# Blocks for the second token group, nine products ahead of the first, and largest logits spread through memory, with a new plan of places and ranks

## The chip, the cores and the metric

The kernel runs on one core of one Trainium2 chip. The metric is the device time of one execution in microseconds (us): less is better. Three runs of the kernel before took 664.44, 664.75 and 665.0 us, so the median is 664.75. The core's TensorE clock as granted was 0.997 of full speed in the profiled execution.

The engines are named as the profile names them: PE (TensorE, matrix products), DVE (VectorE), ACT (ScalarE), POOL (GpSimd) and SP (SyncE, which here only issues transfers).

## What is computed

All values are f32. x is [4, 2048, 256]: 4 sequences of 2048 tokens. Cut to what matters, the reference is:

```
q, k, v = gelu(x W1 + b1) W2 + b2            # three small MLPs, 256 wide
scores  = tril(q k^T) / scale                # no softmax
out     = layernorm(scores v) * ln_w + ln_b
x       = layernorm(x + out)
xn      = layernorm(x) * gamma + beta
logits  = unit(xn) . unit(mu)                # 256 columns: 16 experts x 16 slots
dispatch = softmax(logits, over the tokens of a sequence)
combine  = softmax(logits, over the 256 columns)
slot_in  = dispatch^T xn ; h = gelu(slot_in w1 + b1) ; slot_out = h w2 + b2
x        = layernorm(x + combine slot_out)
```

The attention is linear, so it can be run as a sum that is carried along (k^T v). The dispatch softmax needs, for each of the 256 columns, the largest logit over all 2048 tokens of a sequence. The code keeps logits with their sign turned, so it looks for the least.

## The kernel before

**Tiling.** Tokens are taken in 16 groups of 512 (4 chunks of 128 partitions), 4 groups to a sequence. For each group t, attend (L774) brings x into a transposed form xT, makes q, k and v, the products of k and q, the running state and the attention output; norms (L1018) does the layer norms; back (L1137) makes the logits and the combine weights. After the fourth group of a sequence, softmaxes (L1232) and slots (L1333) do the dispatch and the experts, and finish (L1447) adds the result for each of the four groups and stores it.

**How the order of work is made.** Nothing is run where it is written. Each piece of work is a step of a planner (class Plan, L56): an engine, a length, what it reads and writes, and a rank. The rank is the base given by the last plan.begin(...) plus 0.01 for each step, and it is less by 1.5 for a step that reads a PSUM bank (L93). Plan.run (L119) plays the steps with these lengths and with lateness by engine (LATE, L58; PATIENCE, L61, says how much a rank weighs against being ready, for SP alone), and emits them in the order that comes out. Each engine then runs its own list in that order and waits on semaphores. Buffers are handed out in the same play from a number of places for each tag (L263 to L292): for example hid 5 (the gelu outputs of q, k and v), vt 1, kt 1, xT 2. PSUM has three sets of banks (L299 to L301): mm 3, tp 2, at 3.

**The start.** load_x (L304) loads a group of x as rows. For t of 2 and more it also loads the same group by blocks, 8 transfers of 64 KB each (emit_blocks, L330), which attend turns into xT with one DVE transposition (L782). For groups 0 and 1 attend transposes the rows on PE instead (transpose_group, L489, whose PE step is L481), and copies the two banks with DVE (L471) and ACT (L472). Weights arrive by transfers issued at once (load_weights, L368); the planner is told when to expect them by the list of arrivals. The expert weights w1, w2 and b2 are queued on SP (load_experts, L389). fold (L723) joins W2q and W2k: transpositions of both on PE (L733), copies (L741), three products (L755), and three evictions on DVE (L765) into wqk_sb, which the kt products (L820) read. unit_mu (L686) scales mu; it uses spread.

**A group.** PE makes q, k and v (L797, two tiles of 512 columns each), ACT applies gelu (L807), then the kt products (L820, evicted by DVE at L830) and v's second product (L847, evicted at L858). kt is turned through memory: stored by SP (turn_out, L507, issue at L513), read back in blocks (turn_in, L518, issue at L522) and transposed on DVE (L529) before its products with q (L872). The carried state is L899 (evicted at L915), the column sums are L932, which ACT copies (L941), SP stores (L947) and reads back for all partitions (L952, L956). The outputs are L982 and L986. The logits are L1166, their running least is mx (L1188).

**The end of a sequence.** softmaxes transposes mx on PE (L1241), DVE reduces it to cm, two columns of 128 partitions (L1249), and spread (L666) brings these 256 values to all partitions: DVE multiplies the identity by each column (L672), PE multiplies a matrix of ones by that (L678), ACT copies the bank (L1266). POOL then subtracts it from the logits of each group (L1277; SUBTRACT at L23 says which engine for the very last group's chunks), ACT applies Exp (L1289), and the slot sums on PE (L1311) contract over all tokens. The experts are L1363, L1387, L1406 and L1433, the last product is L1537 (combine, L1530), added by DVE at L1545. For the last two sequences finish_by_sums (L1504) gets the norm from an accumulated sum and a square on ACT (L558), then a root on POOL (root_of, L565: L573, L582, L587, L588, L589), then a centering on ACT (L604) or DVE (L609), as CENTERS (L21) says. PIECES (L19) cuts the last group into chunks; the piece marked True is normed by finish_own (L1461) with DVE's own statistics (L548, L549), a root on POOL (L537) and a centering at L1480. store is L1490.

The last sequence is treated apart: its first three groups are summed early (part_sums), and spread is called for them and once more for the last group.

Of the kernel before, what the change touches and what calls it, by code (L numbers as in the profile page):

```python
# [14 lines left out]
P = 128  # L15
G = 4
ACCZ = 14

PIECES = ((2, False), (2, True))  # L19

CENTERS = [['ACT', 'ACT', 'ACT', 'ACT'], ['ACT', 'DVE', 'DVE', 'DVE'], ['ACT', 'ACT', 'ACT', 'ACT'], ['DVE', 'DVE', 'DVE', 'DVE'], ['ACT', 'DVE', 'ACT', 'DVE'], ['ACT', 'DVE', 'DVE', 'DVE'], ['ACT', 'ACT', 'ACT', 'ACT'], ['DVE', 'DVE', 'ACT', 'DVE']]  # L21

SUBTRACT = ['DVE', 'POOL', 'DVE', 'POOL']  # L23

TAIL = {'norms': 0, 'back': 0.3, 'softE': 1.4, 'part': 2.2, 'soft': 1.0, 'slots2': 4.6, 'fin2': [5.5, 0.3], 'slots3': 1.7, 'fin3': [2.6, 0.2], 'table': 1.0}
LAST = 2
# [29 lines left out]
class Plan:  # L56
# [1 line left out]
    LATE = {"PE": 0.45, "DVE": 0.25, "ACT": 0.25, "POOL": 0.25, "SP": 3.5, "IN": 0.0}  # L58
    TABLE = 1.3

    PATIENCE = {"PE": 0.0, "DVE": 0.0, "ACT": 0.0, "POOL": 0.0, "SP": 1.0, "IN": 0.0}  # L61

    def __init__(self):
        self.steps, self.places, self.order, self.free = [], {}, {}, set()
# [155 lines left out]
def kernel(  # L220
# [36 lines left out]
        plan.tag(tag, tiles, free=math.prod(shape) < 32 or tag == "ct")  # L257

    def bank_places(tag, n):
        plan.tag(f"ps_{tag}", [banks.tile([P, 512], F32, name=f"{tag}_{i}") for i in range(n)], True)  # L260

    for tag, n, shape in (
        ("row", 8, [G, C + 1]),  # L263
        ("xT", 2, [KC, W]),
        ("hid", 5, [KC, W]),
        ("kT", 1, [KC, W]),
        ("vt", 1, [G, C]),
        ("kt", 1, [G, C + 1]),
        ("sT", 1, [G, P]),
        ("a", 2, [G, C]),  # L270
        ("run", 2, [C]),
        ("cs", 1, [C]),
        ("state", 3, [KC, C]),
        ("xn", 2, [G, C]),
        ("xnT", 1, [KC, W]),
        ("lg", 7, [G, ES]),
        ("mx", 1, [ES]),
        ("ct", 5, [EH, W]),
        ("dg", 1, [EH, P]),
        ("si", 1, [EH, C]),  # L280
        ("siT", 1, [KC, ES]),
        ("hp", 1, [NP, S]),
        ("st", 7, [G, 6]),
        ("mv", 14, [G, 2]),
        ("ve", 10, [G]),
        ("root", 24, [G]),
        ("ss", 6, [G]),
        ("nrm", 4, [G]),
        ("sum", 12, [G]),
        ("re", 12, [G]),  # L290
        ("rc", 6, [1]),
        ("cm", 6, [EH]),  # L292
    ):
        places(tag, n, shape)
    plan.tag(
        "bounce", [memory.tile([KC, W, P], F32, name=f"bounce_{i}") for i in range(16)], True
    )
    plan.tag("sums", [memory.tile([G, C], F32, name=f"sums_{i}") for i in range(2)], True)
    bank_places("mm", 3)  # L299
    bank_places("tp", 2)  # L300
    bank_places("at", 3)  # L301


    x_tiles, xs_tiles = {}, {}  # L304

    def load_x(t):
        if t >= ngroups:
            return
        b, g = divmod(t, NG)
        xt = plan.buffer("row", G)  # L310

        def emit():
            nc.sync.dma_start(
                out=xt[:, :, :C],
                in_=x[b, g * W : (g + 1) * W, :].rearrange("(c p) d -> p c d", p=P),
            )
            if t == 0:
                load_weights()
            if t == 1:
                load_rows()  # L320

        plan.step("SP", {0: 2.5, 1: 6.0, 2: 4.0}.get(t, 0.5), emit, writes=[xt])
        x_tiles[t] = xt
        if t < 2:
            return


        xs = plan.buffer("xT", KC)

        def emit_blocks():  # L330
            xb = x[b, g * W : (g + 1) * W, :].rearrange(
                "(n c) (k a r) -> a c k n r", c=32, k=KC, r=32
            )
            for a in range(P // 32):
                for k in range(KC):
                    nc.sync.dma_start(
                        out=xs[32 * a : 32 * (a + 1), k, :].rearrange(
                            "c (n r) -> c n r", r=32
                        ),
                        in_=xb[a][:, k],  # L340
                    )

        plan.step("SP", 4.8, emit_blocks, writes=[xs])
        xs_tiles[t] = xs
# [72 lines left out]

    arrivals = {}
    for n, after in (
        ("W1q", 7.0), ("W1k", 0.5), ("W1v", 1.0), ("muw", 0.5), ("W2q", 0.5), ("W2k", 0.5),  # L420
        ("W2v", 1.0), ("rows", 4.0),
    ):
        plan.tag(n, [mu_sb])
        arrivals[n] = plan.buffer(n)
        plan.step("IN", after, lambda: None, [], [arrivals[n]])
# [28 lines left out]
        pattern=[[1, P]],  # L454
        channel_multiplier=-1,
    )

    hz_t = const.tile([P, NP, 2, S], F32, name="hz")
    nc.gpsimd.memset(hz_t, 0.0)
# [772 lines left out]
    def softmaxes(groups, before=None):  # L1232
# [22 lines left out]
        if before:  # L1255
# [3 lines left out]
                nc.vector.tensor_tensor(less.place, cm.place, before.place, ALU.subtract)  # L1259

            plan.step("DVE", 0.3, emit, [before], [cm, less])
        row = spread(cm)
        cmb = plan.buffer("dg")
        plan.step(
            "ACT", _act(ES),
            lambda: nc.scalar.copy(cmb.place.rearrange("p h e -> p (h e)"), row[:, :ES]),  # L1266
            [row], [cmb],
        )
        for t in groups:

            n = 1 if t == ngroups - 1 else G
# [293 lines left out]
    for t in range(ngroups):  # L1565
# [3 lines left out]
        last = t == ngroups - 1  # L1569
        plan.begin(t)  # L1570
        attend(t)
        plan.begin(t + (TAIL["norms"] if last else 0.6))
        norms(t)
        plan.begin(t + 0.3)
        load_x(t + 2)
        plan.begin(t + (TAIL["back"] if last else 1.1))
        back(t)
        if t == ngroups - 2:

# [5 lines left out]
            kept = part_sums(early)  # L1585
        if t % NG == NG - 1:
            groups = [t] if tail == 2 else list(range(t - NG + 1, t + 1))
            plan.begin(t + (TAIL["soft"] if tail == 2 else 1.4))
            _, less = softmaxes(groups, cm if tail == 2 else None)
            plan.begin(t + (1.7, TAIL["slots2"], TAIL["slots3"])[tail])  # L1590
            so = slots(groups, kept if tail == 2 else None, less)
# [50 lines left out]
```

## Time and profile before

| what | value |
|---|---|
| median of three runs | 664.75 us |
| the profiled execution | 665.03 us |
| its span, first to last instruction | 663.3 us |
| PE busy | 645.4 us, 97% of the span |
| DVE, POOL, ACT busy | 493.4, 298.8, 266.3 us |
| transfers of the hardware queue q1 | 83.06 MB, 59.8% of what 16 DMA engines have in the span |
| first PE product | at 5.88 us |
| PE busy in 0 to 10, 10 to 20, 20 to 30, 30 to 40 us | 4.12, 10.0, 10.0, 9.36 us |
| DMA share in 10 to 20 and 20 to 30 us | 1.00 and 1.17 |
| PE busy from 650 us to the end | 5.63 us |

The span is counted from the first to the last instruction of the profiled execution; 1.7 us of that execution's time lie outside it. A line of the profile names the engine, the line of the code, the operation, the tiles out<-in with their shape, how often, the busy time and the time of one, and the idle time before it with what ended it. In the order of time, a line gives the start, the time that the merged run of like instructions spans, and in brackets the idle time of that engine before it. SPq and ACTq are the issues of transfers, which take the issuing engine's time only. PEld is the load of weights into PE, which runs beside products. An f32 product of the code shows as two records.

### The profile page before, as it was taken

The page shows a single profiled execution, that of the slowest core. Times are in us where ns is not written, and L with a number is a line of the kernel's source. Part 1 is how long each engine was busy: PE and PEld are TensorE (multiplying, and loading weights), DVE is VectorE, ACT ScalarE, POOL GpSimd, SP SyncE. Part 2 cuts the span into 40 slices and gives each one's busy share as a digit, 9 for nine tenths or more (in the row PEclk, how much of TensorE's full clock was granted, in tenths as well). Part 3 has the DMA queues.
Part 4 walks back from the last instruction along what each step waited for, and adds up shares of the span by engine and source line. Part 5 has one row for each costly group of instructions (what it writes and reads, how often), then busy time and mean ns, then how long its engine had stood idle before and what let it go on. Part 6 is the DMA issues. An engine that isn't in the chain of part 4 may idle for free.

```text
span 663.3 us, 9332 instructions
## 1 busy us (share of the span) xinstructions
PE 645.4 (97%) x2954; PEld 479.4 (72%) x2954; DVE 493.4 (74%) x1294; ACT 266.3 (40%) x597; POOL 298.8 (45%) x346
## 2 busy tenths in 40 slices
PE   6999999999999999999999999999999999999995
PEld 3757586777768877758686887776867768887874
DVE  1438586979797878878796388996969589886486
ACT  3130415243346227221516323624153545545475
POOL 3443516060739414353426605546061937646234
PEclk9999999999999999999999999999999999999998
DMA  8953655877677095836676425995677382621284
GB/s 245 261 118 103 139 91 133 128 151 153 108 152 128 8 212 164 189 88 128 127 142 123 87 64 95 234 211 104 111 149 132 70 159 68 84 65 32 33 159 159
DMA packets 322233, 84.71 MB, mean 128 GB/s; under 512 B 253068, under 2 KB 319944, under 8 KB 322184
## 3 DMA queue, kind: packets, MB, share of 16 engines
q1 hardware_dynamic: 321080, 83.06, 59.8%
q10 hardware_dynamic: 960, 0.80, 0.4%
q8 instruction: 23, 0.38, 0.2%
q0 software_dynamic: 144, 0.26, 0.1%
q14 instruction: 26, 0.21, 0.1%
HBM read 52.05 MB, written 32.04 MB: 127 GB/s over the span
## 4 chain that ended last, share of the span: by engine, by line
PE 91%; DVE 5%; issue 1%; DMA 1%; POOL 0%; POOLq 0%; ACT 0%; DVEq 0%; ACTq 0%
PE mm L797 25%; PE at L899 8%; PE mm L847 8%; PE mm L1166 8%; PE at L1537 7%; PE at L982 7%; PE mm L820 7%; PE at L1311 7%; PE at L872 4%; PE at L986 4%; PE at L932 1%; DVE mx L1188 1%; DMA row<-in_x_dram 1%; PE tp L481 1%; DVE xn L1091 1%
## 5 line engine op out<-in xcount | busy, mean ns | idle before, releaser
L807 ACT ACTIVATE hid<-mm,cols_sb 128x512 f32<-128x512 f32 x96 | 65.1, 687 | 139.2 <-PE mm L797 138.7
L537 POOL TENSOR_TENSOR root<-ve,nhalf 128x4 f32<-128x4 f32 (+1 forms) x39 | 40.6, 1041 | 127.8 <-DVE ve L1032 51.5
L982 PE MATMUL at<-state,hid 128*128 128x256 f32 x240 | 61.7, 379 | 0.0
L797 PE MATMUL mm<-xT,W1q_sb 128*128 128x512 f32 x128 | 61.3, 608 | 0.3 <-DVE xT L471 0.3
L899 PE MATMUL at<-vt,kt 128*128 128x256 f32 x240 | 61.4, 386 | 0.0
L820 PE MATMUL mm<-both_sb,hid 128*128 128x257 f32 x256 | 59.5, 381 | 1.3 <-DVE kt L830 1.3
L797 PE MATMUL mm<-xT,W1v_sb 128*128 128x512 f32 x128 | 59.4, 592 | 0.0
L1537 PE MATMUL at<-so,ct 128*128 128x256 f32 x256 | 58.0, 381 | 0.8 <-DVE row L1545 0.6
L1311 PE MATMUL at<-row,lg 128*128 128x257 f32 x256 | 58.2, 380 | 0.0
L847 PE MATMUL mm<-W2v_sb,hid 128*128 128x256 f32 x256 | 58.1, 379 | 0.0
L1166 PE MATMUL mm<-mu_sb,xnT 128*128 128x256 f32 x256 | 58.1, 379 | 0.0
L797 PE MATMUL mm<-xT,W1k_sb 128*128 128x512 f32 x128 | 57.8, 593 | 0.0
L1537 PEld LDWEIGHTS at<-so,ct 128*128 128x128 f32 x256 | 48.0, 190 | 10.0 <-issue 1.7
L820 PEld LDWEIGHTS mm<-both_sb,hid 128*128 128x128 f32 x256 | 48.2, 190 | 9.7 <-DVE kt L830 1.9
L1166 PEld LDWEIGHTS mm<-mu_sb,xnT 128*128 128x128 f32 x256 | 48.4, 190 | 8.4 <-issue 1.4
L1025 POOL TENSOR_TENSOR row<-row,rows_sb 128x1024 f32<-128x1024 f32 x16 | 35.1, 2196 | 42.7 <-DMA row<-in_x_dram 38.1
L982 PEld LDWEIGHTS at<-state,hid 128*128 128x128 f32 x240 | 45.5, 190 | 12.2 <-issue 6.0
L847 PEld LDWEIGHTS mm<-W2v_sb,hid 128*128 128x128 f32 x256 | 48.4, 190 | 6.9 <-DVE kt L830 0.3
L1311 PEld LDWEIGHTS at<-row,lg 128*128 128x128 f32 x256 | 48.1, 190 | 7.2 <-issue 0.4
L899 PEld LDWEIGHTS at<-vt,kt 128*128 128x128 f32 x240 | 44.3, 190 | 12.3 <-issue 5.4
L1216 POOL TENSOR_TENSOR sum<-sum,ss 128x4 f32<-128x4 f32 x16 | 4.0, 249 | 108.6 <-DVE ss L1212 92.2
L941 ACT COPY cs<-at 128x256 f32<-128x256 f32 (+1 forms) x16 | 5.9, 371 | 109.3 <-PE at L932 97.7
(148 smaller groups left out, 1247.5 us busy)
## 6 DMA issues: line engine op xcount, KB each, us to landing
bounce<-xn SPq DMA_DIRECT2D x30, 512.0 KB
row<-in_x_dram SPq DMA_DIRECT2D x16, 512.0 KB
ct<-bounce SPq DMA_DIRECT2D x64, 128.0 KB
bounce<-kt SPq DMA_DIRECT2D x30, 256.0 KB
kT<-bounce SPq DMA_DIRECT2D x60, 128.0 KB
out_dram<-row SPq DMA_DIRECT2D x15, 512.0 KB
xT<-in_x_dram SPq DMA_DIRECT2D x112, 64.0 KB
xnT<-bounce SPq DMA_DIRECT2D x56, 128.0 KB
```

Of the source, the lines that this page charges most:

```text
L537: nc.gpsimd.tensor_tensor(r[:, :n], v[:, :n], nhalf.to_broadcast([P, n]), ALU.pow)
L797: nc.tensor.matmul(ph.place, wa[f"W1{n}"][:, k, m * P : (m + 1) * P], xT[:, k, :], start=(k == 0), stop=(k == KC - 1),)
L807: nc.scalar.activation(hid[n][:, m, :], ph.place, AF.Gelu, bias=cols_sb[:, 4 * i + m : 4 * i + m + 1],)
L820: nc.tensor.matmul(pk[:, : C + 1], hid["k"][:, k, c * P : (c + 1) * P], wqk_sb[:, k, :], start=(k == 0), stop=(k == KC - 1),)
L847: nc.tensor.matmul(pv[:, j * C : (j + 1) * C], hid["v"][:, k, (c0 + j) * P : (c0 + j + 1) * P], wa["W2v"][:, k, :], start=(k == 0), stop=( ...
L872: nc.tensor.matmul(psc[:, toks[c]], kT[:, k, toks[c]], qT[:, k, toks[c]], start=(k == 0), stop=(k == KC - 1),)
L899: nc.tensor.matmul(pds[:, m * C : (m + 1) * C], kt[:, c, m * P : (m + 1) * P], vt[:, c, :], start=True, stop=True,)
L982: nc.tensor.matmul(po[:, :C], qT[:, k, toks[c]], s[:, k, :], start=(k == 0), stop=False,)
L1025: lambda: nc.gpsimd.tensor_tensor(row[:, :, :C], row[:, :, :C], lnb_r, ALU.add),
L1166: nc.tensor.matmul(pl[:, j * ES : (j + 1) * ES], xnT[:, k, (c0 + j) * P : (c0 + j + 1) * P], mu_sb[:, k, :], start=(k == 0), stop=(k == KC ...
L1311: nc.tensor.matmul(psi[:, : C + 1], lg[:, c, h * P : (h + 1) * P], row[:, c, :], start=(i == 0), stop=(i == n - 1),)
L1537: nc.tensor.matmul(pc[:, :C], ct[:, h, c * P : (c + 1) * P], so_t[:, h, :], start=(h == 0), stop=(h == EH - 1),)
```

## The change

It has these parts.

1. Group 1 is loaded by blocks like the later groups (`t < 1` for `t < 2`), so its xT comes from a DVE transposition and not from PE.
2. Nine products of the identity by itself are issued on PE ahead of everything else, into a bank of at that is used later. Nothing reads them.
3. The planner's list of arrivals is changed: W2q 2.0 for 0.5, W2k 0.1 for 0.5, rows 3.0 for 4.0. The transfers themselves are issued as before. The steps of fold are so placed later.
4. For the three sequences before the last, the least logits are spread through memory: SP stores cm's 256 values as 4-byte elements to a tile mins in DRAM, and reads it back for all 128 partitions. spread stays for the last sequence and for mu.
5. The last group is cut into pieces of 2, 1 and 1 chunks, of which the last is normed by finish_own.
6. Places, ranks and engines: hid 4 for 5, vt 2 for 1, SP's PATIENCE 1.5 for 1.0, the bases of norms, load_x, back and softmaxes, and the lists CENTERS and SUBTRACT.

Since the order is the planner's, all four lists of instructions come out in another order. With the lines of before: in PE's list group 0's second q tile stands ahead of L733, and k's tiles ahead of L755; in DVE's list the first L782 stands ahead of the three L765.

```diff
@@ -16,11 +16,11 @@
 G = 4
 ACCZ = 14
 
-PIECES = ((2, False), (2, True))
-
-CENTERS = [['ACT', 'ACT', 'ACT', 'ACT'], ['ACT', 'DVE', 'DVE', 'DVE'], ['ACT', 'ACT', 'ACT', 'ACT'], ['DVE', 'DVE', 'DVE', 'DVE'], ['ACT', 'DVE', 'ACT', 'DVE'], ['ACT', 'DVE', 'DVE', 'DVE'], ['ACT', 'ACT', 'ACT', 'ACT'], ['DVE', 'DVE', 'ACT', 'DVE']]
-
-SUBTRACT = ['DVE', 'POOL', 'DVE', 'POOL']
+PIECES = [(2, False), (1, False), (1, True)]
+
+CENTERS = [['ACT', 'ACT', 'DVE', 'ACT'], ['ACT', 'DVE', 'DVE', 'ACT'], ['ACT', 'ACT', 'ACT', 'ACT'], ['DVE', 'DVE', 'DVE', 'DVE'], ['ACT', 'DVE', 'ACT', 'DVE'], ['ACT', 'DVE', 'DVE', 'ACT'], ['DVE', 'ACT', 'ACT', 'DVE'], ['ACT', 'DVE', 'ACT', 'DVE']]
+
+SUBTRACT = ['POOL', 'DVE', 'DVE', 'DVE']
 
 TAIL = {'norms': 0, 'back': 0.3, 'softE': 1.4, 'part': 2.2, 'soft': 1.0, 'slots2': 4.6, 'fin2': [5.5, 0.3], 'slots3': 1.7, 'fin3': [2.6, 0.2], 'table': 1.0}
 LAST = 2
@@ -58,7 +58,7 @@
     LATE = {"PE": 0.45, "DVE": 0.25, "ACT": 0.25, "POOL": 0.25, "SP": 3.5, "IN": 0.0}
     TABLE = 1.3
 
-    PATIENCE = {"PE": 0.0, "DVE": 0.0, "ACT": 0.0, "POOL": 0.0, "SP": 1.0, "IN": 0.0}
+    PATIENCE = {"PE": 0.0, "DVE": 0.0, "ACT": 0.0, "POOL": 0.0, "SP": 1.5, "IN": 0.0}
 
     def __init__(self):
         self.steps, self.places, self.order, self.free = [], {}, {}, set()
@@ -257,14 +257,16 @@
         plan.tag(tag, tiles, free=math.prod(shape) < 32 or tag == "ct")
 
     def bank_places(tag, n):
-        plan.tag(f"ps_{tag}", [banks.tile([P, 512], F32, name=f"{tag}_{i}") for i in range(n)], True)
+        tiles = [banks.tile([P, 512], F32, name=f"{tag}_{i}") for i in range(n)]
+        plan.tag(f"ps_{tag}", tiles, True)
+        return tiles
 
     for tag, n, shape in (
         ("row", 8, [G, C + 1]),
         ("xT", 2, [KC, W]),
-        ("hid", 5, [KC, W]),
+        ("hid", 4, [KC, W]),
         ("kT", 1, [KC, W]),
-        ("vt", 1, [G, C]),
+        ("vt", 2, [G, C]),
         ("kt", 1, [G, C + 1]),
         ("sT", 1, [G, P]),
         ("a", 2, [G, C]),
@@ -295,10 +297,11 @@
     plan.tag(
         "bounce", [memory.tile([KC, W, P], F32, name=f"bounce_{i}") for i in range(16)], True
     )
+    plan.tag("mins", [memory.tile([EH, P], F32, name=f"mins_{i}") for i in range(2)], True)
     plan.tag("sums", [memory.tile([G, C], F32, name=f"sums_{i}") for i in range(2)], True)
     bank_places("mm", 3)
     bank_places("tp", 2)
-    bank_places("at", 3)
+    at_banks = bank_places("at", 3)
 
 
     x_tiles, xs_tiles = {}, {}
@@ -321,7 +324,7 @@
 
         plan.step("SP", {0: 2.5, 1: 6.0, 2: 4.0}.get(t, 0.5), emit, writes=[xt])
         x_tiles[t] = xt
-        if t < 2:
+        if t < 1:
             return
 
 
@@ -417,8 +420,8 @@
 
     arrivals = {}
     for n, after in (
-        ("W1q", 7.0), ("W1k", 0.5), ("W1v", 1.0), ("muw", 0.5), ("W2q", 0.5), ("W2k", 0.5),
-        ("W2v", 1.0), ("rows", 4.0),
+        ("W1q", 7.0), ("W1k", 0.5), ("W1v", 1.0), ("muw", 0.5), ("W2q", 2.0), ("W2k", 0.1),
+        ("W2v", 1.0), ("rows", 3.0),
     ):
         plan.tag(n, [mu_sb])
         arrivals[n] = plan.buffer(n)
@@ -454,6 +457,9 @@
         pattern=[[1, P]],
         channel_multiplier=-1,
     )
+
+    for _ in range(9):
+        nc.tensor.matmul(at_banks[0][:, :P], ident, ident, start=True, stop=True)
 
     hz_t = const.tile([P, NP, 2, S], F32, name="hz")
     nc.gpsimd.memset(hz_t, 0.0)
@@ -1259,13 +1265,30 @@
                 nc.vector.tensor_tensor(less.place, cm.place, before.place, ALU.subtract)
 
             plan.step("DVE", 0.3, emit, [before], [cm, less])
-        row = spread(cm)
-        cmb = plan.buffer("dg")
-        plan.step(
-            "ACT", _act(ES),
-            lambda: nc.scalar.copy(cmb.place.rearrange("p h e -> p (h e)"), row[:, :ES]),
-            [row], [cmb],
-        )
+        if groups[-1] < ngroups - 4:
+            mins, cmb = plan.buffer("mins"), plan.buffer("dg")
+            plan.step(
+                "SP", 0.6,
+                lambda: nc.sync.dma_start(
+                    out=mins.place.rearrange("h p -> p h"), in_=cm.place
+                ),
+                [cm], [mins],
+            )
+            plan.step(
+                "SP", 0.5,
+                lambda: nc.sync.dma_start(
+                    out=cmb.place, in_=mins.place.partition_broadcast(P)
+                ),
+                [mins], [cmb],
+            )
+        else:
+            row = spread(cm)
+            cmb = plan.buffer("dg")
+            plan.step(
+                "ACT", _act(ES),
+                lambda: nc.scalar.copy(cmb.place.rearrange("p h e -> p (h e)"), row[:, :ES]),
+                [row], [cmb],
+            )
         for t in groups:
 
             n = 1 if t == ngroups - 1 else G
@@ -1569,11 +1592,11 @@
         last = t == ngroups - 1
         plan.begin(t)
         attend(t)
-        plan.begin(t + (TAIL["norms"] if last else 0.6))
+        plan.begin(t + (TAIL["norms"] if last else 0.7))
         norms(t)
-        plan.begin(t + 0.3)
+        plan.begin(t + 0.5)
         load_x(t + 2)
-        plan.begin(t + (TAIL["back"] if last else 1.1))
+        plan.begin(t + (TAIL["back"] if last else 1.2))
         back(t)
         if t == ngroups - 2:
 
@@ -1585,7 +1608,7 @@
             kept = part_sums(early)
         if t % NG == NG - 1:
             groups = [t] if tail == 2 else list(range(t - NG + 1, t + 1))
-            plan.begin(t + (TAIL["soft"] if tail == 2 else 1.4))
+            plan.begin(t + (TAIL["soft"] if tail == 2 else 1.2))
             _, less = softmaxes(groups, cm if tail == 2 else None)
             plan.begin(t + (1.7, TAIL["slots2"], TAIL["slots3"])[tail])
             so = slots(groups, kept if tail == 2 else None, less)
```

## The prediction, made before the changed kernel ran

> **What bounds the kernel now.** I read the share of each engine first, then TensorE's waits, then the order of time at the start, at the end of the first sequence, and at the end of the run.
>
> ```profile
> PE 645.4 (97%) x2954; PEld 479.4 (72%) x2954; DVE 493.4 (74%) x1294; ACT 266.3 (40%) x597; POOL 298.8 (45%) x346
> ```
>
> TensorE is the bound, so time can come from four places: less work on it, a faster clock, fewer stalls, or a shorter stretch before its first and after its last product. The waits that the profile admits are few:
>
> ```profile
> PE tp L481 <- DMA row<-in_x_dram: 5.9, 1, 5.9
> PE mm L820 <- DVE kt L830: 1.3, 1, 1.3
> PE at L932 <- DVE vt L858: 0.9, 1, 0.9
> ```
>
> The busy figure hides more. I took the interval of each kind of product from long runs in the chain (0.43 us for a record 512 wide, 0.216 for 256 wide, 0.111 for 128 wide, 0.109 for a transposition; one product in the code is two records) and multiplied by the counts in program order: 632.4 us of work. The span of 663.3 less 5.9 before the first product and 7.7 after the last (ended near 655.6) leaves 649.7. So 17.3 us are lost in between. The cold clock is 2.6 of them; 14.7 are gaps. Comparing start times with the running sum places these: 3.2 up to 62 us, 0.7 near 230, 1.9 at 276 to 297, 2.6 at 397 to 449, 1.4 before 611; the rest is about 0.2 a group.
>
> The start, where the reader is to compare like with like: 8 transpositions cold and warm, 4 products cold and warm, and one load that waits for a transfer.
>
> ```profile
> 5.88 1.94 PE L481 MATMUL tp<-ident,row 128*128 128x128 f32 x8 [5.88 <-DMA row<-in_x_dram]
> 7.75 3.59 PE L797 MATMUL mm<-xT,W1q_sb 128*128 128x512 f32 x4
> 11.17 0.85 PEld L733 LDWEIGHTS tp<-ident,both_sb 128*128 128x128 f32 x8 [1.21 <-DMA both_sb<-in_W2q_dram]
> 12.10 1.88 PE L797 MATMUL mm<-xT,W1q_sb 128*128 128x512 f32 x4
> ...
> 17.93 1.25 DVE L782 STREAM_TRANSPOSE xT<-xT 128x1024 f32<-128x1024 f32 x1
> ...
> 34.39 1.07 PE L481 MATMUL tp<-ident,row 128*128 128x128 f32 x8
> ```
>
> The end of the first sequence: the largest logits (L1241) are ready to spread, PE spreads them, POOL subtracts for 9.71 us, and the slot sums (L1311) follow 13 us after L1241, with PE at other work until then.
>
> ```profile
> 197.75 0.38 PE L1241 MATMUL tp<-ident,mx 128*128 128x128 f32 x2
> 201.69 0.60 PE L678 MATMUL mm<-dg,ones 128*128 128x256 f32 x2
> 203.50 9.71 POOL L1277 TENSOR_TENSOR lg<-lg,dg 128x1024 f32<-128x1024 f32 x4
> 210.75 14.08 PE L1311 MATMUL at<-row,lg 128*128 128x257 f32 x64
> ```
>
> **What the Trainium skill says.** (1) "TensorE: Matmul & The Clock Gate", Part 1: the array's clock is halved by default and freed by about 3.4 us of activity in a free-running window. This trace agrees: 1.94 us against 0.87 to 1.07 for the same 8, 3.59 against 1.88; the slow stretch ends between 10.5 and 11.3, some 5 us after the first product. (2) "DMA: Bandwidth & Descriptors", Specifications: below 512 B an element a transfer leaves line rate. The new store moves 4-byte elements; no row here shows that. (3) "Perfetto Trace Analysis", Tensor Engine Instruction (MATMUL, LD_WEIGHTS): ACT, DVE and GpSimd are strict FIFO, and PE's ends are estimated. Agrees: the second L858 stood behind a waiting L1042 on DVE and cost PE 0.9.
>
> **The change part by part.** Sums are against the profiled execution (665.03, span 663.3, 1.7 outside it), which is 0.3 above the median of 664.75.
>
> *Nine products of ident by ident.* Each is 0.22 us warm (as L872), so 2.0 in all, twice that cold. ident is ready at 1.36 and x at 5.88, so 4.0 cold fits with 0.4 to spare: free. It should have the clock up at 5.88. Worth 2.6 alone: 1.94-0.87 plus 3.59-1.88, less 0.2 of other waiting.
>
> *Later fold.* With a warm clock PE would reach L733 at 8.9 but W2q lands at 11.17. The new order puts q's second tile first (1.72): both are done by 10.6, and PE waits only 0.6. At 11.2 it is one tile, 1.7 us, ahead.
>
> *Where that lead goes.* After L733 (0.87) and k (3.44) the fold's three products run from 15.5 to 18.1. In the new DVE order the transposition of group 1's blocks stands ahead of all three evictions of the fold (L765). The blocks are the same 8 transfers at the same place in SP's queue that served group 2 before; the last small packets move at 17.0, and DVE ran L782 at 17.93. So DVE is held until 17.7 or so, evicts the first fold product at 19.0 to 19.4, and PE, whose v tile needs that bank, stands from 18.1 to 19.4. Then v takes 3.44, and the kt products (L820) start near 22.95 against 23.29 before. Gain 0.3; if the blocks land by 15.5 it is 1.7; if at 18.5, a loss of 0.5. I take 0.3.
>
> *Group 1 as blocks.* Off PE go 8 transpositions, 0.87, and the waits of that place: from 33.36 to 40.34 PE had 5.5 us of work and lost 1.2 to the xT copies and to dg; two q and two k tiles now stand ahead of dg, so I take 1.0. DVE gets a 1.25 transposition for a 0.69 copy, ACT loses a 0.59 copy. SP issues 8 transfers more (4.4 to 8.9 us of issue); group 2's blocks move behind w1, kt's store behind them (about 28 to 29), then the loads of kT, and w2 and b2 behind those. kT's products come 20 us of work after L820, near 43.8; kT's loads leave SP by 36 and land 2.2 later (40.07 to 42.2 before). Covered by 4 us. w2 and b2 are first used near 237.
>
> *Largest logits by memory, three times.* Off PE 3 x 0.43 = 1.3; off DVE 6 x 0.36 and off ACT 3 x 0.37, hidden there. The new route: L1249's result, a store on SP, its landing, a read for all partitions, its landing. The nearest row is sums<-cs: issued 70.03, next issue that waits for it 72.19, so 2.2; the broadcast of a took 4.2 from issue to POOL's start (191.7 to 195.9), and the new one is a third as large but queued behind it. From L1241: 2.3 (transposition, DVE's turn, reduction), 2.3, 0.5, 3.5 to 4.2: POOL starts 8.6 to 9.3 after it, against 5.75 before. Four subtractions (9.7) and an Exp (1.1) end at 20. The new order has 15.4 and 15.8 us of PE work between L1241 and the slot sums at the first two sequences (12.7 and 13.6 before), and the fourth group is needed 5 and 6 us later: 20.4 and 21.9. At the third, 68 us. So just covered; I take a loss of 0.4 for both, with 0 and 6 as ends. SP's queue: the store waits for DVE ahead of the cb loads, the next xT blocks and xnT; these have over 10 us.
>
> *Places and ranks.* hid 5 to 4, vt 1 to 2, other ranks. No work changes; the 14.7 of gaps can move either way. Seen in the lists: both vt evictions now stand together where L1042 split them at 285 (the wait of 0.9). The kt stall at 61 keeps its DVE order, so it stays. Removable gaps sum to about 6.5 outside the start, so the ends are a gain of 4 and a loss of 3; I take a gain of 0.5.
>
> *Last group in 2, 1, 1.*
>
> ```profile
> 657.51 0.81 POOL L537 TENSOR_TENSOR root<-ve,nhalf 128x2 f32<-128x2 f32 x1 [0.50 <-DVE ve L1470]
> 658.35 0.74 DVE L1480 TENSOR_SCALAR row<-row,mv,root 128x256 f32<-128x256 f32 x2 [0.26 <-POOL root L537]
> ```
>
> The last chunk saves a bn pair and a center (0.9), but two centers of the group before stand ahead of it on DVE (0.74): ready near 658.8 for 659.1. The third chunk's root now queues on POOL behind the last one's: four steps, 1.4, from 658.4, then ACT 0.55: 660.45. Its store is half as large (0.36). Transfers ended at 661.3 before, about 661.6 now: a loss of 0.3, ends -0.4 and +0.7.
>
> *Sum:* -0.3 -0.87 -1.0 -1.3 +0.4 -0.5 +0.3 = -3.3. 665.03 - 3.3 = 661.7; on the median, 661.5.
>
> **The rivals.**
> A, forecast: 661.5 (659.8 to 663.3).
> B, faster still: the blocks land in time, so the lead of 1.7 stays (1.4 more), and the new places remove 2 more of the gaps. For: 6.5 us of gaps are there. Against: DVE's first-in order and the 17.9. 664.75-3.3-1.4-1.6 = 658.5.
> C, no change: hid with 4 places and q no longer run ahead leave PE nothing to do while ACT and DVE evict; 3 us of new gaps of the size now at 280. 664.5.
> D, slower: the route through memory. The fourth Exp must end by 20.4 and 21.9 after L1241, so POOL must start by 9.6 and 11.1; each us beyond is a us of idle PE. From a start 12.2 after L1241 on, the two stalls (2.6 and 1.1) offset the 3.7 that the rest gains; at 13.2, with 4-byte elements and SP busy, 3.6 + 2.1 = 5.7, so 664.75-3.7+5.7 = 666.7. Against: 2.2 for the like store.
> E, the nine products don't free the clock (window out of step): no lead to lose, so 0.3 more, 661.8; inside A.
>
> **How the numbers follow.** A with E 0.50, B 0.25, C 0.15, D 0.10. About 0.2% (1.3 us) is what a measurement of this kernel tells from no change: A and B faster, C the same, D slower. The range holds A and most of B and half of C: 657.5 to 664.8, the ends of the places' bounds mostly inside.
>
> **What would show it.** Right: 8 transpositions in 0.9 to 1.0 us at 5.9; PE idle near 18 to 19.4 on DVE; no L481 at 34; L820 at 23; POOL's first subtraction 9 us after L1241 and the slot sums with no gap; a last store near 660.5. Wrong: 1.9 us for those 8 (E); no stall at 18 (B); gaps inside the slot sums on ACT's Exp (D); the loss from last product to end below 7 us; gaps by group that grow past 0.5 (C).

## The result, and the profile after

The changed kernel takes 673.1 us (median of 4 runs, 672.66 to 673.45); the kernel before, beside it, 664.6 (664.28 to 665.0). The ratio of the two is 1.0128, with a 95% interval from 1.0113 to 1.0143: slower, where 661.5 was forecast. The profiled execution of after has a span of 671.3 us.

Line numbers are those of after from here on: L487 was L481, L803 L797, L826 L820, L1247 L1241, L1300 L1277, L1312 L1289, L1334 L1311, L788 L782, L771 L765; in the experiments they shift by a few more. First the engines' line of its page, to hold against the one shown of before:

```profile
PE 648.8 (97%) x2958; PEld 482.0 (72%) x2958; DVE 489.0 (73%) x1287; ACT 262.7 (39%) x594; POOL 297.7 (44%) x350
```

By this line nothing happened: all shares are within a point. TensorE's waits say more; the columns are the total, the number and the longest in us:

```profile
PE at L1334 <- DVE a L1003: 5.2, 1, 5.2
PE at L1334 <- ACT lg L1312: 1.8, 3, 0.9
```

Both lines are of the slot sums, and neither has a like in before. The order of time shows the first, at the end of the first sequence. A line gives the start, the time of the merged run, the engine, and in brackets the idle time before it:

```profile
190.42 0.38 PE L1247 MATMUL tp<-ident,mx 128*128 128x128 f32 x2
191.29 0.38 SPq L1272 DMA_DIRECT2D mins<-cm  x1
191.72 0.46 SPq L958 DMA_DIRECT2D a<-sums  x1
199.84 0.32 SPq L1279 DMA_DIRECT2D dg<-mins  x1
200.26 5.61 SPq L528 DMA_DIRECT2D ct<-bounce  x4
204.31 0.73 POOL L972 TENSOR_TENSOR a<-a,run 128x256 f32<-128x256 f32 x1 [5.89 <-DMA a<-sums]
205.80 9.46 POOL L1300 TENSOR_TENSOR lg<-lg,dg 128x1024 f32<-128x1024 f32 x4
208.17 1.06 ACT L1312 ACTIVATE lg<-lg 128x1024 f32<-128x1024 f32 x1 [5.75 <-POOL lg L1300]
209.49 1.25 DVE L535 STREAM_TRANSPOSE ct<-ct 128x1024 f32<-128x1024 f32 x1 [6.62 <-DMA ct<-bounce]
211.19 16.13 PE L1334 MATMUL at<-row,lg 128*128 128x257 f32 x64 [5.25 <-DVE a L1003]
```

SP stores the least logits at 191.29 and can issue the read that waits for them only at 199.84, 8.55 us later, where 2.2 was forecast (the delay from a store to the issue that waits for it is called its landing here). At the other two sequence ends it is 7.64 (360.10 to 367.74) and 9.07 (520.42 to 529.49). The read of the sums, issued 0.4 after the store, is late too: 12.6 us to POOL's start at L972, which stands ahead of the first subtraction on POOL. The loads of ct stand behind the read on SP, DVE stands for them 6.62, and with it L1003, which frees the bank that the slot sums need. So PE idles 5.25, and then its 64 records take 16.13 for the 14.08 of before. The stretches of 6 us after 200 say why they take longer; the columns are the bounds, the length, PE busy, PEld, DVE, ACT and POOL busy, the granted clock, the DMA share and GB/s:

```profile
200.00:206.00 6.00, 5.94 (x28) 4.89 (x26) 2.00 (x5) 2.37 (x6) 1.61 (x3) 1.00 0.60 144
206.00:212.00 6.00, 0.81 (x2) 0.75 (x3) 2.48 (x4) 2.11 (x2) 6.00 (x3) 0.70 1.05 175
212.00:218.00 6.00, 6.00 (x21) 4.92 (x21) 2.59 (x4) 2.11 (x2) 5.84 (x6) 0.73 0.90 134
218.00:224.00 6.00, 6.00 (x29) 5.21 (x29) 3.21 (x7) 0.00 (x0) 0.07 (x1) 1.00 0.00 0
```

PE was busy throughout 212 to 218, at a clock of 0.73: after the stand of 5.25 the slow clock costs 2.05 more, while the page's busy shares hide it as work. Of the 5.25, POOL's late chain alone would have kept PE for 3.3: the first Exp, behind the first subtraction, ended only at 209.23 (208.17 and 1.06). The rest is ct's.

**The account.** As in the forecast, the sum of PE's work in program order is taken off the start time of an instruction; the difference, in us, is what has been lost so far (the total of work is 632.4 before, 632.2 after). The last two columns are experiments told below.

| lost so far at | before | after | pairs | rows |
|---|---|---|---|---|
| first kt products (L826) | 8.6 | 6.1 | 8.8 | 5.6 |
| first end, transposition (L1247) | 13.0 | 8.0 | 11.8 | 8.6 |
| first end, after the slot sums | 13.3 | 15.5 | 12.0 | 9.5 |
| second end, L1247 | 16.6 | 18.1 | 14.2 | 12.1 |
| second end, after the slot sums | 16.7 | 21.2 | 16.0 | 14.0 |
| third end, L1247 | 20.3 | 24.8 | 18.9 | 17.6 |
| third end, after its slot sums (some 95 us later) | 22.0 | 30.5 | 22.1 | 20.9 |
| last combine products | 22.9 | 31.3 | 22.9 | 21.8 |

After arrives at the first end with a lead of 5.0. The three ends then cost 7.5, 3.1 and 5.7 where before they cost 0.3, 0.1 and 1.7: 14.2 us. The lead of 5.0 and 0.7 gained between the ends go against that: 14.2-5.0-0.7 = 8.5, by which it is behind at the last products (8.4 in the table, by rounding).

### The profile page after: what moved, and what is told of

It is laid out like the page before. It is cut to its first block, busy times and chain, and to the rows that moved or that the text cites. A ratio compares the mean times of both kernels' runs of the same rounds, so it can differ in the third digit from the quotient of the medians.

```text
span 671.3 us, 9363 instructions
## 1 busy us (share of the span) xinstructions
PE 648.8 (97%) x2958; PEld 482.0 (72%) x2958; DVE 489.0 (73%) x1287; ACT 262.7 (39%) x594; POOL 297.7 (44%) x350
## 4 chain that ended last, share of the span: by engine, by line
PE 80%; DVE 7%; DMA 7%; POOL 2%; SPq 2%; issue 1%; ACT 0%; DVEq 0%; POOLq 0%; ACTq 0%
PE mm L803 21%; PE at L1560 8%; PE at L905 7%; PE mm L853 7%; PE mm L1172 7%; PE mm L826 6%; PE at L988 6%; PE at L1334 6%; PE at L878 4%; PE at L992 3%; DMA mins<-cm 2%; SPq L528 2%; PE at L938 1%; POOL lg L1300 1%; DVE mx L1194 1%
## 5 line engine op out<-in xcount | busy, mean ns | idle before, releaser
L1334 PE MATMUL at<-row,lg 128*128 128x257 f32 x256 | 61.0, 391 | 7.0 <-DVE a L1003 5.2
L826 PE MATMUL mm<-both_sb,hid 128*128 128x257 f32 x256 | 59.6, 382 | 1.6 <-DVE kt L836 1.2
L1334 PEld LDWEIGHTS at<-row,lg 128*128 128x128 f32 x256 | 49.0, 195 | 16.5 <-issue 6.0
L803 PE MATMUL mm<-xT,W1v_sb 128*128 128x512 f32 x128 | 59.8, 593 | 0.8 <-DVE both_sb L771 0.8
L1172 PE MATMUL mm<-mu_sb,xnT 128*128 128x256 f32 x256 | 58.5, 379 | 1.1 <-DVE xnT L535 1.1
L1205 ACT ACTIVATE xn<-lg,nrm 128x256 f32<-128x256 f32 x64 | 31.9, 500 | 69.7 <-DVE lg L1182 69.6
L803 PE MATMUL mm<-xT,W1q_sb 128*128 128x512 f32 x128 | 59.0, 597 | 0.2 <-DVE xT L477 0.2
L803 PE MATMUL mm<-xT,W1k_sb 128*128 128x512 f32 x128 | 58.0, 592 | 0.0
L826 PEld LDWEIGHTS mm<-both_sb,hid 128*128 128x128 f32 x256 | 48.1, 190 | 12.6 <-issue 2.9
L1172 PEld LDWEIGHTS mm<-mu_sb,xnT 128*128 128x128 f32 x256 | 48.4, 190 | 9.3 <-DVE xnT L535 1.5
L988 PEld LDWEIGHTS at<-state,hid 128*128 128x128 f32 x240 | 45.5, 190 | 12.1 <-issue 5.3
L889 DVE SCALAR_TENSOR_TENSOR sT<-at,kt,mask 128x128 f32<-128x128 f32 x64 | 18.0, 343 | 40.2 <-PE at L878 40.2
```

The source lines that it names most:

```text
L803: nc.tensor.matmul(ph.place, wa[f"W1{n}"][:, k, m * P : (m + 1) * P], xT[:, k, :], start=(k == 0), stop=(k == KC - 1),)
L826: nc.tensor.matmul(pk[:, : C + 1], hid["k"][:, k, c * P : (c + 1) * P], wqk_sb[:, k, :], start=(k == 0), stop=(k == KC - 1),)
L988: nc.tensor.matmul(po[:, :C], qT[:, k, toks[c]], s[:, k, :], start=(k == 0), stop=False,)
L1172: nc.tensor.matmul(pl[:, j * ES : (j + 1) * ES], xnT[:, k, (c0 + j) * P : (c0 + j + 1) * P], mu_sb[:, k, :], start=(k == 0), stop=(k == KC ...
L1205: nc.scalar.activation(by_halves(cb)[:, :, c, :], lg[:, c, :].rearrange("p (h e) -> p h e", h=EH), AF.Exp, bias=nrm[:, c : c + 1], scale=-1.0,
L1334: nc.tensor.matmul(psi[:, : C + 1], lg[:, c, h * P : (h + 1) * P], row[:, c, :], start=(i == 0), stop=(i == n - 1),)
```

## The experiments

**Theories.** S: the store of 256 single elements takes some 8 us to be seen as done, and what stands behind it on SP, POOL and DVE makes the loss. R, the rival: the new places, ranks and patience put transfers late, and the store only shows it. T, on the part before the first end: the lead at the start is eaten by DVE's order.

**Route set back, route added, rows: with a new plan.** Three kernels changed the steps that the planner gets:

```
e1_spread_again      -        if groups[-1] < ngroups - 4:   (store and read)
                     +        row = spread(cm)               (all sequences)
e2_before_by_memory  before, with the store and the read of after
e4_two_rows          + plan.step("PE", _FLIP, ... nc.tensor.transpose(flip[:EH, :P], cm.place, ident) ...)
                     + plan.step("DVE", 0.25, ... nc.vector.tensor_copy(wide[:EH, :], flip[:EH, :P]) ...)
                     + plan.step("SP", 0.6, ... nc.sync.dma_start(out=mins.place, in_=wide[:EH, :]) ...)
```

> The changed kernel with only the route of the largest logits set back: all sequences spread them by DVE, PE and ACT again. Theory S (the store of 256 single elements takes some 8 us, and SP, DVE and POOL stand behind it): the three sequence ends give back 13.5 us less the 1.3 us of PE work that returns, so 673.1-13.5+1.3 = 660.9, between 659 and 663. Rival R (the new places, ranks and SP's patience put transfers late; the store only shows it): little comes back, 670 or more.

> The kernel before with only the memory route added. Theory S: the same 13.5 us are lost less 1.3 us of PE work saved, 664.6+12.2 = 676.8, between 672 and 680, with the read of the least logits again 7.5 to 9 us behind their store. Rival R: with the places and ranks of before the route is covered as in the forecast's term, 663.5 to 665.

> The changed kernel, but the two columns of least logits are first turned by one PE transposition and a DVE copy into two rows of 128, so that the store moves 2 pieces of 512 bytes instead of 256 of 4. Theory S with the cause in the size of the elements: the read is issued 2 to 3 us after the store as with the sums, POOL starts its subtractions some 9 to 10 us after the transposition of the running least, and the time is near the forecast, 661 to 663. If a route through memory is slow at any element size: the read still 7 us or more behind the store, 670 or more. Rival R: 670 or more with a store of 2 to 3 us.

Measured, with the ratio to before and its interval: 690.07 (1.0401, 1.0380 to 1.0421), 688.8 (1.0392, 1.0365 to 1.0419) and 678.27 (1.0224, 1.0201 to 1.0247). Read as they stand, the first and third speak for R. They don't: all three plays of the planner gave other lists on all engines. The waits of TensorE with two rows:

```profile
PE at L1466 <- ACT hz L1458: 4.8, 1, 4.8
PE tp L488 <- DVE xnT L1159: 2.5, 1, 2.5
PE tp L1439 <- DVE si L1430: 1.8, 1, 1.8
```

None is at a sequence end of the first three; the 4.8 is of the last experts, and the run with spread has the same 4.8. With rows the running loss is 18.0 at 587 us (before: about 21 there), and 36.2 at the end: 18 of its loss fall in the last group, whose ranks fit one order of steps. So one change of a step moves up to 18 us elsewhere, and these runs decide nothing on the total. What stays of them is the landing: with two rows the read was issued 3.1, 2.7 and 2.3 us behind the store; with single elements in the plan of before 10.6, 10.5 and 9.1.

**Pairs, in the order of after.** The steps stay as they are, so the lists of all engines are those of after, row for row; only the tile in memory is turned, and POOL reads its second operand with a stride.

```
-    plan.tag("mins", [memory.tile([EH, P], ...
+    plan.tag("mins", [memory.tile([P, EH], ...
-                    out=mins.place.rearrange("h p -> p h"), in_=cm.place
+                    out=mins.place, in_=cm.place
```

> The changed kernel with the tile in memory laid out partition by partition, so that the store moves 128 pieces of 8 bytes instead of 256 of 4 (the read stays one contiguous 1 KB row, POOL's second operand is read with a stride of 2). If the store's time goes by the number of pieces: 2.2 plus half of the 6.4 us above it, some 5.4 us, and the time about 665 to 668. If it is a fixed cost of small writes: 7.5 us or more still, and 671 to 674.

Measured: 662.76, ratio 0.9985 (0.9975 to 0.9994). Half the pieces, of 8 bytes, are worth 9.5 us on the ratios, and the time is 2 below the range expected from the number of pieces. Number and size of the pieces change together, so which of them counts is not shown. The same place as above in this kernel's order of time:

```profile
194.31 0.38 PE L1247 MATMUL tp<-ident,mx 128*128 128x128 f32 x2
195.18 0.34 SPq L1272 DMA_DIRECT2D mins<-cm  x1
198.77 0.32 SPq L1277 DMA_DIRECT2D dg<-mins  x1
204.27 9.83 POOL L1310 TENSOR_TENSOR lg<-lg,dg 128x1024 f32<-128x1024 f32 x4
209.67 14.11 PE L1340 MATMUL at<-row,lg 128*128 128x257 f32 x64
```

3.59 for 8.55 (2.88 and 4.85 at the other ends); POOL starts 10.0 after the transposition, and the slot sums run without a gap in 14.11. R as the cause of the 14.2 is out: with the same order and the same places the three ends cost 0.2, 1.8 and 3.2.

**Spread, and rows, in the order of after.** Both are put into the places of the two SP steps without telling the planner.

```
e6_spread_held  SP's store -> two DVE products of ident by cm, into a tile of their own
                SP's read  -> a PE product with ones into the free half of L1247's bank, an ACT copy
e12_rows_held   SP's store -> PE transposition of cm, DVE copy, store of [2, 128]; the read stays
```

> The changed kernel in its own order of instructions, held fixed: only the two transfers of the three sequence ends are replaced, by two DVE products, one PE product and an ACT copy at their places. Theory S: no read stands in SP's queue, so the 13.5 us at the three ends come back less 1.3 us of PE work: 660.9, between 660 and 664, near the run with pairs. If the new places and ranks lose by themselves: 666 or more.

> The changed kernel in its own order, held fixed: at the place of the store a PE transposition and a DVE copy turn the least logits into two rows, and the store moves 2 pieces of 512 bytes. If the number of pieces (or their size) alone sets the landing: read 2.3 to 3.1 us behind the store, POOL no later than with pairs, 662 to 664. If the earlier run with rows lost its 15 us by the route and not by its other order of the last group: 675 or more.

Measured: spread 663.2, ratio 0.9996 (0.9981 to 1.0011); rows 662.69, ratio 0.9983 (0.9975 to 0.9990). As S has it, three routes that are not 256 single elements give the same time within 0.9 us on the ratios. With rows:

```profile
191.06 0.38 PE L1248 MATMUL tp<-ident,mx 128*128 128x128 f32 x2
193.61 0.25 SPq L1275 DMA_DIRECT2D mins<-wide  x1
194.84 0.38 SPq L1284 DMA_DIRECT2D dg<-mins  x1
200.52 9.51 POOL L1305 TENSOR_TENSOR lg<-lg,dg 128x1024 f32<-128x1024 f32 x4
```

The read follows the store by 1.23 (1.11 and 1.26 at the other ends): even below the 2.2 that the forecast took from another store. SP shows no wait before it, so this is a bound on the landing from above. What rows gain in landing, the turn ahead of the store takes (2.55 from its L1248 to the store, for 0.87).

**The route in the order of before.** The store takes the place of spread's DVE step, the read that of ACT's copy, PE's product is left out; nothing else moves.

```
-                nc.vector.tensor_scalar(dg[:, h, :], ident, col[:, h : h + 1], None, ALU.mult)
+                nc.sync.dma_start(out=mins.rearrange("h p -> p h"), in_=col.place)   # e8: out=mins
-            nc.scalar.copy(cmb..., row[:, :ES])
+            nc.sync.dma_start(out=cmb.place, in_=mins.partition_broadcast(P))
```

> The kernel before in its own order, held fixed: at the three sequence ends the store of 256 single elements takes the place of the DVE products of spread, the read that of the ACT copy, and the PE product is gone. Theory S: POOL starts 13 to 15 us after the transposition of the running least, the fourth Exp ends 24 to 26 us after it, where the slot sums of that order want it at 18 and 20; 6 us are lost at each of the first two ends, 1 to 3 at the third, less 1.3 us of PE work: 672 to 680. Rival (the cost came from the new order): 663 to 666.

> As the run before, with pairs of 8 bytes: the read is issued 3 to 5 us behind the store, POOL starts 9 to 10 us after the transposition, the fourth Exp ends at 20 to 21 where 18 and 20 are wanted: 2.5 and 1 us lost, 1.3 us of PE work saved, so 664 to 667. That would say that the route gains nothing in the order of before even with a quick store, and that the changed order (slot sums 2 to 3 us later) was made for it.

Measured: single elements 691.86 (1.0417, 1.0396 to 1.0437), pairs 678.02 (1.0210, 1.0180 to 1.0240). Both lose 11 to 12 more than the ends of their expected ranges. The slot sums of the first end, with pairs:

```profile
212.60 2.01 PE L1329 MATMUL at<-row,lg 128*128 128x257 f32 x8 [2.53 <-ACT lg L1307]
215.13 2.01 PE L1329 MATMUL at<-row,lg 128*128 128x257 f32 x8 [0.52 <-ACT lg L1307]
217.49 2.01 PE L1329 MATMUL at<-row,lg 128*128 128x257 f32 x8 [0.35 <-ACT lg L1307]
219.83 8.97 PE L1329 MATMUL at<-row,lg 128*128 128x257 f32 x40 [0.34 <-ACT lg L1307]
```

The 2.5 was expected; the three waits after it and what follows were not. By the account the ends cost 5.1, 5.9 and 7.7, while 0.3, 0.1 and 1.7 was the price of before. The read was issued 5.85, 6.89 and 6.28 behind the store, later than with pairs in the order of after: at the first end SP was busy with the four ct loads from 200.09 to 205.42, which stand between the two in this list, so 5.85 is no landing. So with pairs the route costs next to nothing in one of the two orders tried and 13.7 in the other; that the later slot sums of the first give it the time fits, but was not tried alone. The step from single elements to pairs is worth 13.8 here. With single elements the first slot sums wait 9.33 on Exp and the end costs 11.8.

**The read issued by POOL.** It waits for the result anyway, so this should have freed SP.

```
-                lambda: nc.sync.dma_start(
+                lambda: nc.gpsimd.dma_start(
                     out=cmb.place, in_=mins.place.partition_broadcast(P)
```

> The changed kernel in its own order, held fixed, store of single elements as it is, but the read of the least logits is issued by POOL, which waits for it anyway, so that nothing stands behind the waiting read in SP's queue. If most of the loss is SP's queue (the ct, xT and xnT transfers behind the read, DVE behind them): boundary 1 loses 3 to 4 instead of 7.4, boundary 3 nothing instead of 2.9, boundary 2 as it was: 665 to 669. If it is POOL's late start alone: 672 to 674.

Measured: 680.74 (1.0244, 1.0214 to 1.0275), worse than after itself; neither outcome was right. POOL's own list at the first end, with SP's loads of ct and their user on DVE:

```profile
193.87 14.60 SPq L528 DMA_DIRECT2D ct<-bounce  x4
202.58 0.63 POOL L1279 DMA_DIRECT2D dg<-mins  x1 [5.48 <-DMA mins<-cm]
203.24 2.37 POOL L1115 TENSOR_TENSOR xn<-xn,rows_sb 128x1024 f32<-128x1024 f32 x1
206.51 0.73 POOL L972 TENSOR_TENSOR a<-a,run 128x256 f32<-128x256 f32 x1 [0.90 <-DMA a<-sums]
209.84 9.47 POOL L1300 TENSOR_TENSOR lg<-lg,dg 128x1024 f32<-128x1024 f32 x4 [1.81 <-DMA dg<-mins]
211.39 1.25 DVE L535 STREAM_TRANSPOSE ct<-ct 128x1024 f32<-128x1024 f32 x1 [5.49 <-DMA ct<-bounce]
```

The wait went from SP to POOL, and L1115 and L972, which had run in its shadow, stand behind it now; the store itself landed no sooner (10.2, 10.8 and 8.5). POOL starts 18.3 after the transposition and PE waits 6.28 for Exp, so here PE's stand ends with POOL. But ct came late as well: its loads, with no waiting read ahead of them on SP, took 14.60 to issue (5.61 in after, 3.88 with rows), and DVE stood 5.49 for them. So taking the read out of SP's list does not free what stands behind the store. How much of after's 14.2 is the queue and how much POOL stays open beyond the first end.

**The start: evictions first, and without the nine products.** All three are the kernel with pairs, lists held.

```
e9   DVE: L771 x3, then L788 of group 1      (after: L788, then L771 x3)
e11  -    for _ in range(9):
     -        nc.tensor.matmul(at_banks[0][:, :P], ident, ident, start=True, stop=True)
e13  both
```

> The kernel with pairs in its own order, held fixed, but in DVE's list the three evictions of the fold stand ahead of the transposition of group 1's blocks. Theory T (the transposition waits for transfers, PE stands behind it for 0.8 to 2.4 us near 18 us, and a stand of 2 us costs up to 1.8 more by the clock): the stand and the cold stretch after it are gone, the kt products start near 21.9, and 1 to 2.5 us are gained on the 662.8 with pairs: 660.3 to 661.8. If another wait takes its place: 662.3 to 663.

> The kernel with pairs in its own order, without the nine products at the start. If the stand behind DVE near 18 to 20 us swallows what they gain, as the forecast had it: PE comes to that place 2 us later, waits less there and keeps a warm clock, and the time stays within 0.5 of 662.8. If they are worth their 2.6 us to the end: 665 to 665.5.

> Both edits: evictions of the fold ahead of the transposition, and no nine products. With no stand to swallow it, the slow clock at the start counts in full: 2 to 2.6 us above the run with the evictions first, so 662.5 to 664. If the nine products are worth nothing: the same as that run.

Measured: evictions first 661.32, ratio 0.9966 (0.9953 to 0.9979), the best of all kernels here; without the nine 663.98 (1.0001, 0.9988 to 1.0014); both 663.3 (0.9986, 0.9977 to 0.9995). So the order on DVE is worth 1.3 on the ratios, and the nine products 1.1 with the stand and 1.3 without it (2.0 by the medians of that comparison). Each of these differences is about as large as its own 95% interval (1.1 us to either side, from those of the two ratios), so their sizes are rough, and without the nine the time fell between the two outcomes named. The start with pairs, PE and DVE:

```profile
17.28 1.03 PE L761 MATMUL mm<-row,cols_sb 128*128 128x257 f32 x4
18.64 1.25 DVE L788 STREAM_TRANSPOSE xT<-xT 128x1024 f32<-128x1024 f32 x1 [5.41 <-DMA xT<-in_x_dram]
20.25 5.40 PE L803 MATMUL mm<-xT,W1v_sb 128*128 128x512 f32 x8 [1.94 <-DVE both_sb L771]
25.49 3.64 PE L826 MATMUL mm<-both_sb,hid 128*128 128x257 f32 x16
```

and with the evictions first:

```profile
16.97 1.03 PE L763 MATMUL mm<-row,cols_sb 128*128 128x257 f32 x4
17.84 3.60 PE L810 MATMUL mm<-xT,W1v_sb 128*128 128x512 f32 x8
18.51 1.25 DVE L778 STREAM_TRANSPOSE xT<-xT 128x1024 f32<-128x1024 f32 x1
21.27 3.64 PE L833 MATMUL mm<-both_sb,hid 128*128 128x257 f32 x16
```

In the first the blocks came at 18.6, PE stood 1.94, and the same 8 records took 5.40 instead of 3.60; in the windows of that run the clock from 22 to 26 is 0.64. The kt products start 4.2 later. So T's mechanism is seen, but these two executions overstate its worth: the one with pairs took 664.57 (median 662.76), the other 659.88 (median 661.32). The granted clock was 0.995 in that one and one more of the 20 with pairs, 0.996 to 0.998 in the other 18, which fits that most of them did not have the slow stretch; the worth is the 1.3.

## Why the prediction was wrong, step by step

- *Memory route, +0.4.* This step failed: 0.4 was forecast, with 6 as the far end, and the three ends cost 14.2 more than before. Its price for the landing, 2.2, came from `sums<-cs`, a store of 4 rows of 256; the size of the pieces was noted beside it and then left out of the price. Measured: 8.55, 7.64 and 9.07 with 256 pieces of 4 bytes, 2.9 to 4.9 with 128 of 8, 1.1 to 1.3 with 2 of 512 (2.3 to 3.1 in the run with a new plan). With pairs the rest of the step comes out as forecast: POOL starts 10.0 and 9.9 after L1247 at the first two ends (limits forecast: 9.6 and 11.1), and the slot sums have no gap from the route. In part that is luck: from L1247 to the store it is 0.87 and not 2.3, which makes up for 5.5 from the read to POOL's start where 4.0 to 4.7 were forecast. The like transfer was misread too: the read of a was issued at 191.02 (191.77 is that of run), so it took 4.8 and not 4.2.
- *Rival D, 666.7.* Its mechanism, its condition and its sign are what happened, and it put the start of POOL at 13.2 (measured 15.4, 13.4 and 13.6). It came out 6.4 low for three reasons, all left out of it: the loads behind the read in SP's list (said to have over 10 us; DVE stood 6.62 for ct), the clock after the stand (2.05), and the third end, which was said to have 68 us. At the third end Exp was indeed not late: ct, xnT and kt came late (the L1172 products waited 1.14 for xnT, L938 0.52 for vt behind ct on DVE).
- *Start, -0.3.* The stand on DVE at 18 is real: 0.77 in after, 1.94 with pairs, 2.41 with spread held. In after the kt products start at 22.74 for 22.95 forecast. But the bound "0.5 lost if the blocks land at 18.5" was wrong: landing at 18.6 cost 2.2 against before (25.49 for 23.29), as the cold clock after the stand was not in it. The 8 transpositions took 1.66 in after, where the clock was freed at 7.0, near their end; they took 1.09 to 1.11, not 0.9 to 1.0, in three others, where it was freed at 4.4 to 5.6.
- *Group 1 as blocks, -0.87 and -1.0.* As forecast: no L487 at 34; the q tiles follow L705 without a wait.
- *Places and ranks, -0.5.* Better: the kt stall at 61, said to stay, is gone in after (1.3 and what followed it), and the lead at the first end is 5.0. Between the ends after loses 2.6 and 3.6, before 3.3 and 3.6. The rest is inside the bounds given. The forecast's "waiting L1042" in before was not waiting: it ran 1.70 (the next one 0.45) while POOL's L1025 ran.
- *Tail, +0.3.* From the end of the last product to the end of the span: 7.4 (663.9 to 671.3), 7.7 before: a gain of 0.3 where a loss of 0.3 was forecast.
- *The sum.* Without the failed step the forecast's -3.3 is to be held against pairs, -1.0, and rows, -1.1 on their ratios: 2 too good, of which 1.3 come back with the evictions first (-2.3). Two slips in its sums change nothing in it: the gaps that it placed add up to 9.8 of 14.7, which leaves 0.3 a group and not 0.2, and rival B names 2 more of the gaps but takes off 1.6. One of the gaps that is left stands at the second end: PE waits 1.45 for L836 on DVE with pairs, 1.39 with rows, not with spread held. With pairs, L836 stood behind two L1015 that took 1.80 and 1.49 while POOL subtracted; none of the 32 L1015 of that trace beside which POOL ran nothing took over 0.49. That POOL's work holds up DVE's was not tested, and the gap near 440 is unexplained.

## What to carry to other kernels

Price a transfer by a row with pieces of the same size and number, not only the same bytes; if no row has it, its landing is the widest bound of the sum, and the store of a column to memory is better turned into rows or pairs first. Where PE is made to stand for more than about 1.7 us, add a possible slow clock after the stand, and ask what stands behind the waiting instruction in every list that it is in. When a planner sets the order, hold the lists fixed before a part is tried alone: the same route, spread, gave 690 with a new plan and 663 in the order held.

## What the runs showed of the hardware

The store's bytes were not what took the time. Of after, windows of the DMA record from 191.5 to 193, 193 to 195, 196 to 198 and 202 to 204 us:

```profile
DMA packets 472, 0.10 MB, mean 64 GB/s; under 512 B 288, under 2 KB 472, under 8 KB 472
...
DMA packets 0, 0.00 MB, mean 0 GB/s; under 512 B 0, under 2 KB 0, under 8 KB 0
...
DMA packets 10, 0.03 MB, mean 15 GB/s; under 512 B 0, under 2 KB 0, under 8 KB 10
...
DMA packets 291, 0.47 MB, mean 237 GB/s; under 512 B 28, under 2 KB 191, under 8 KB 291
```

The small packets, enough of them for all 256 pieces, had passed by 193. Then nothing moved for 2 us, and the read of the sums, behind the store in the same queue, moved 28 packets in the 7 us from 195 to 202, with the engines otherwise idle. It took 12.6 from issue to its user on POOL, and 5.1 with rows, where POOL did not wait for it. The Trainium skill ("DMA: Bandwidth & Descriptors", Anatomy of one DMA) puts most of a fixed cost of about 2 us, for transfers that GpSimd issues, down to the memory's receipt for the write. These stores are SP's: rows (1.1 to 1.3) are below that figure, single elements are some four times as long, and they hold back a read issued after them. That it is the receipts that queue up is an inference; the trace shows only the silence and the trickle.

The clock fell after shorter stands than expected. "TensorE: Matmul & The Clock Gate", Part 1, puts the slow state after an idle window of about 3.4 us; here stands of 1.94 and 2.41 near 20 us were each followed by 5.40 for 3.60, while the 2.53 of the run with pairs in the order of before left the clock at 1.00. The clock record has the reason: in each of the 14 traces the clock changes only at whole steps of 3.41 us from its first change. These are two such steps with pairs, then two about the stand of 2.53:

```profile
18.08:21.50 3.42, 1.48 (x5) 0.68 (x4) 2.22 (x4) 0.00 (x0) 2.23 (x3) 1.00 1.12 316
21.50:24.91 3.41, 3.41 (x5) 1.35 (x4) 0.00 (x0) 0.69 (x1) 3.03 (x4) 0.50 1.21 207
...
208.06:211.47 3.41, 2.01 (x10) 1.43 (x8) 3.31 (x7) 0.00 (x0) 2.38 (x2) 1.00 0.99 215
211.47:214.88 3.41, 2.01 (x8) 1.44 (x8) 0.27 (x1) 1.91 (x2) 3.41 (x2) 1.00 0.68 107
```

The 1.94 lie in one step, the 2.53 are shared between two, and each of these has 1.40 of idle PE. Between the first rise of the clock and the last product, all 18 steps at full clock in which PE idled 1.94 or more were followed by one at 0.50, and none of those with 1.69 or less was; of two between, the one with 1.73 was and the one with 1.76 was not. So, in these traces, it takes about half a step of idle PE. The first change comes at 4.4 to 11.4 us, by the run, so the same stand would cost up to 1.8 us more in one execution and nothing in another; no run here repeats a trace of one kernel to show it.
